# Four Mamba-style layers on one core: images in pairs, convolution by planes through DRAM, outputs in groups of two chunks

## The chip, the cores and the metric

The kernel runs on one core of one Trainium2 chip, in float32 throughout. The metric is the device time of one launch in microseconds, the median of three runs. One core has TensorE (PE: matrix products, with its weight loads shown as PEld), VectorE (DVE), ScalarE (ACT), GpSimd (POOL) and SyncE (SP, which issues the DMA transfers here). Each engine runs its own instructions strictly in the order of its program; engines wait for one another through semaphores.

## The reference, cut to what matters

Four images of 64x64 positions and 192 channels go through four layers a, b, c, d. Each layer is a group normalisation, then a selective state-space block, then an addition to the layer's input:

```python
# per layer, one image; L = 64*64 = 4096 positions, 16 states
xn = group_norm(x)                       # 32 groups of 6 channels
u, z = in_proj(xn)                       # 192 -> 384 + 384 (layer c: 192 + 192)
u = silu(depthwise_conv(u) + bias)       # a: 4 taps along the sequence; b, c, d: 3x3
for each direction:                      # a: 4, b: 1, c: 4 (two at a time), d: 4
    s = u in this direction's order      # rows, rows reversed, columns, columns reversed; b: snake
    dt, B, C = x_proj(s)
    delta = softplus(dt_proj(dt) + b)
    h = exp(delta*A)*h + (delta*s)*B     # a recurrence along the sequence, 16 states a channel
    y += (h*C).sum(states) + D*s
# b, c, d: y = layer_norm(y over channels) * silu(z);  a: each direction's y * silu(z of that direction)
x = x + out_proj(y)
```

Layer a has its own input and output projection for each of its four directions, and its output passes a last linear map, which the kernel folds into the output weights. The next layer's group normalisation needs the mean and variance of the whole new x, so a layer of an image cannot start before the same image's layer before it has ended. Different images do not depend on each other at all.

## The kernel before

An image is held as channels on partitions (two halves of 96 channels, 4096 positions along the free axis) and worked on in 8 chunks of 512 positions. Images run one after another, and in each the layers a, b, c, d. Each layer has three parts, in scopes of memory pools that open and close one after the other:

**In** (`stats`, `load_normal`, then `conv1d` for a, `conv` for b, c, d). `stats` turns moments gathered earlier into mean and rstd (two small PE products, one Ln and one Exp on ACT). x is loaded in 8 chunks and normalised on DVE (line 122). For each block of channels PE makes `pu` (lines 175, 231), ACT copies it into a padded plane `pad` (179, 235), and DVE adds the taps: a first `tensor_scalar` and one `scalar_tensor_tensor` for each further tap (159 and 161; 261 and 263). Of the first block some chunks are done on PE instead, as products with diagonal matrices (`pc`, 198 and 253): 6 of 8 chunks for b and d, 5 for c, 2 for a. ACT applies Silu. In b and d the result `xc` stays in SBUF for the scans; in a it is stored to DRAM (`xd_a`, one store for each block), in c in both row and column order from SBUF tiles `xc` and `xt` (line 1016); column order is made in SBUF, so that each run of memory stored is 16 KB.

**Scans** (`scans`). An order written out by hand and pinned by `keep` runs over directions, chunks and pairs of states: `p_px` (413), `p_dbl` (420), a store and broadcast loads of B and C, `p_softplus`, `p_du` (485), `inflow` (588, POOL), `decay` (582 and 584, ACT), `scan` (633, DVE), `outflow` (648, POOL or DVE), `total` (688, PE), `store` (702 and 706). Chunks of xs are loaded from DRAM where the source is there; otherwise `p_px` and `p_du` read `xc` directly, with a stride for column directions.

**Out** (`out0` for a, `output` for b, c, d). `output` makes a first pass over all 8 chunks (load y, for c add two parts; `bn_stats` and `bn_aggr` at 798 and 799; load and normalise x; products `pz` at 807, Silu at 810 into z), then one rsqrt for all chunks, held behind all the Silus by `behind`, and then a second pass over the 8 chunks: normalise y (821), transposes `pg` (828), scale and bias on ACT (838), product with z on POOL (839), products `po` (846), addition of x (850), store, moments for the next group normalisation (70). `out0` is one pass over 8 chunks, each with four directions of `pz` (963), Silu (967), `pg` (970), product on DVE (974) and `po` (931).

Outside `scans` the order of each engine's instructions is made by the scheduler of the framework, which goes by the order in which they are recorded and by when their operands and buffers come free.

Of the kernel before, what the change touches and what calls it, by code (L numbers as in the profile page):

```python
# [27 lines left out]
CONV_ROWS = 16  # L28
CONV_SPLIT = 37
# [17 lines left out]
class Net:  # L47
# [24 lines left out]
    def new_moments(self, key):  # L72
        return self.const.tile([HP, 2, NCH, 6], F32, tag="mom", bufs=2, name=f"mom_{key}")
# [12 lines left out]
    def stats(self, keep, pool, pp, st, key):  # L86

        nc = self.nc
# [3 lines left out]
        ps = pp.tile([HP, 2], F32, tag="gps", bufs=1, name=f"gm_{key}")  # L92
        nc.tensor.matmul(ps, self.gmat, mv[:, :, 0], start=True, stop=True)
        mean = keep.tile([HP, 2], F32, tag="mean", name=f"mean_{key}")
# [6 lines left out]
        ps = pp.tile([HP, 2], F32, tag="gps", bufs=1, name=f"gv_{key}")  # L101
# [3 lines left out]
        rstd = keep.tile([HP, 2], F32, tag="rstd", name=f"rstd_{key}")  # L105
# [23 lines left out]
    def conv(self, pool, pp, xn, xc, sums, P, nb, w_u, cpack, taps, shape, interior, borders, snake, key, xt=None):  # L129

        nc = self.nc
        k = len(taps)
        r0, c0 = interior
        wu = pool.tile([HP, 2, nb * P], F32, tag="wu", name=f"wu_{key}")
        nc.sync.dma_start(wu, w_u)
        cp = pool.tile([P, nb, cpack.shape[-1]], F32, tag="cp", name=f"cp_{key}")
        nc.sync.dma_start(cp, cpack)

        def silu(b, lo, hi, v):
            bias = cp[:, b, k : k + 1]
            o = img(xc[:, b, :])[:, lo:hi, :]
            if snake:
                nc.scalar.activation(o[:, 0::2, :], v[:, 0::2, :], AF.Silu, bias=bias)
                return nc.scalar.activation(o[:, 1::2, ::-1], v[:, 1::2, :], AF.Silu, bias=bias)
            if xt is not None:
                o2 = xt[:, b, :].rearrange("p (w h) -> p h w", h=H)[:, lo:hi, :]
                nc.scalar.activation(o2, v, AF.Silu, bias=bias)
            return nc.scalar.activation(o, v, AF.Silu, bias=bias)  # L150

        done = []

        def on_vector(b, pad, lo, hi):
            acc = img(sums[:, b, :])[:, lo:hi, :]
            for i, (tr, tcol) in enumerate(taps):
                v = pad[:, tr + lo : tr + hi, tcol : tcol + W]
                if i == 0:
                    nc.vector.tensor_scalar(acc, v, cp[:, b, :1], None, ALU.mult)
                else:  # L160
                    nc.vector.scalar_tensor_tensor(  # L161
                        acc, v, cp[:, b, i : i + 1], acc, ALU.mult, ALU.add
                    )
            done.append(silu(b, lo, hi, acc))

        for b in [*range(1, nb), 0]:
            pad = pool.tile([P, *shape], F32, tag="pad", bufs=nb, name=f"pad_{key}{b}")
            for sl in borders:  # L170
                nc.gpsimd.memset(pad[(slice(None), *sl)], 0.0)
            for ch in range(NCH):
                pu = pp.tile([P, T], F32, tag="pu", bufs=4, name=f"pu_{key}{b}{ch}")
                for h in range(2):
                    nc.tensor.matmul(
                        pu, wu[:, h, b * P : (b + 1) * P], xn[:, h, ch * T : (ch + 1) * T],
                        start=h == 0, stop=h == 1,
                    )
                nc.scalar.copy(pad[:, r0 + ch * R : r0 + (ch + 1) * R, c0 : c0 + W], rows(pu))
            if b:  # L180

                half = H // 2 - 1 - snake
                on_vector(b, pad, 0, half)
                on_vector(b, pad, half, H)
                continue
            diag = pool.tile([P, k, P], F32, tag="diag", name=f"dg_{key}")
            nc.vector.tensor_tensor(
                diag,
                self.ident[:P, None, :P].to_broadcast([P, k, P]),
                cp[:, b, :k, None].to_broadcast([P, k, P]),  # L190
                ALU.mult,
            )
            own = 6 if nb > 2 else 5
            on_vector(b, pad, own * R, H)
            for ch in range(own):
                pc = pp.tile([P, T], F32, tag="pc", bufs=3, name=f"pc_{key}{ch}")
                for i, (tr, tcol) in enumerate(taps):
                    nc.tensor.matmul(
                        pc, diag[:, i, :],
                        pad[:, tr + ch * R : tr + (ch + 1) * R, tcol : tcol + W],  # L200
                        start=i == 0, stop=i == k - 1,
                    )
                done.append(silu(b, ch * R, (ch + 1) * R, rows(pc)))
        return done

    def conv1d(self, pool, pp, xn, out, w_u, cpack, cols, rev, key):


        nc = self.nc
        P, nb = 128, 3  # L210
        wu = pool.tile([HP, 2, nb * P], F32, tag="wu", bufs=2, name=f"wu_{key}")
        nc.sync.dma_start(wu, w_u)
        cp = pool.tile([P, nb, 5], F32, tag="cp", bufs=2, name=f"cp_{key}")
        nc.sync.dma_start(cp, cpack)
        taps = [6 - k if rev else k for k in range(4)]
        done = []
        for b in range(nb):
            pad = pool.tile([P, (H + 6) * W], F32, tag="pad", bufs=4, name=f"pad_{key}{b}")
            if cols:
                pad = pad.rearrange("p (h w) -> p h w", w=W)  # L220
                inside = pad[:, 3 : H + 3, :]
                borders = pad[:, :3, :], pad[:, H + 3 :, :]
            else:
                pad = pad.rearrange("p (h w) -> p h w", h=H)
                inside = pad[:, :, 3 : W + 3]
                borders = pad[:, :, :3], pad[:, :, W + 3 :]
            nc.gpsimd.memset(borders[rev], 0.0)
            for ch in range(NCH):
                pu = pp.tile([P, T], F32, tag="pu", bufs=5, name=f"pu_{key}{b}{ch}")
                for h in range(2):  # L230
                    nc.tensor.matmul(
                        pu, wu[:, h, b * P : (b + 1) * P], xn[:, h, ch * T : (ch + 1) * T],
                        start=h == 0, stop=h == 1,
                    )
                nc.scalar.copy(inside[:, ch * R : (ch + 1) * R, :], rows(pu))
            acc = pool.tile([P, L], F32, tag="acc", bufs=2, name=f"acc_{key}{b}")
            xo = pool.tile([P, L], F32, tag="xo", bufs=2, name=f"xo_{key}{b}")
            to = xo.rearrange("p (w h) -> p h w", h=H) if cols else img(xo)
            bias, r0 = cp[:, b, 4:5], 0
            if b == 0:  # L240
                r0 = CONV_ROWS
                diag = pool.tile([P, 4, P], F32, tag="diag", bufs=2, name=f"dg_{key}")
                nc.vector.tensor_tensor(
                    diag,
                    self.ident[:, None, :].to_broadcast([P, 4, P]),
                    cp[:, b, :4, None].to_broadcast([P, 4, P]),
                    ALU.mult,
                )
                for r in range(0, r0, R):
                    pc = pp.tile([P, T], F32, tag="pc", bufs=2, name=f"pc_{key}{r}")  # L250
                    for i, t in enumerate(taps):
                        v = pad[:, t + r : t + r + R, :] if cols else pad[:, r : r + R, t : t + W]
                        nc.tensor.matmul(pc, diag[:, i, :], v, start=i == 0, stop=i == 3)
                    done.append(nc.scalar.activation(to[:, r : r + R, :], rows(pc), AF.Silu, bias=bias))

            for lo, hi in ((r0, CONV_SPLIT), (CONV_SPLIT, H)):
                a = img(acc)[:, lo:hi, :]
                for i, t in enumerate(taps):
                    v = pad[:, t + lo : t + hi, :] if cols else pad[:, lo:hi, t : t + W]
                    if i == 0:  # L260
                        nc.vector.tensor_scalar(a, v, cp[:, b, :1], None, ALU.mult)
                    else:
                        nc.vector.scalar_tensor_tensor(a, v, cp[:, b, i : i + 1], a, ALU.mult, ALU.add)
                done.append(nc.scalar.activation(to[:, lo:hi, :], a, AF.Silu, bias=bias))
            nc.sync.dma_start(out[:, b, :], xo)
        return done

    def conv2d(self, pool, pp, xn, xc, sums, P, nb, w_u, cpack, snake, key, xt):
# [5 lines left out]
            snake, key, xt,  # L274
        )

    def keep(self, ins):

# [890 lines left out]
```

## Time and profile before

| | |
|---|---|
| runs | 30956.24, 30958.65 and 30989.16 us; median 30958.65 us |
| profiled execution | span 30966.4 us, 7.7 us above the median |
| busy share of the span | PE 76%, PEld 57%, DVE 84%, ACT 75%, POOL 79% |
| scan stage of a, b, c, d, first image | 2190.5, 571.9, 1146.0, 2283.2 us |
| from the last scan of a layer to the first scan of the next: a to b, b to c, c to d, d to a | 551.8, 290.8, 263.5, 443.6 us |
| before the first scan of all, after the last scan of all | 306, 152 us |
| DMA | mean 108 GB/s; 1371014 packets, 187576 of them under 512 bytes |

A span is the time from the first to the last instruction of the one execution that was profiled. The busy share of an engine is an average over very different stages: the table's two rows of stages say more. A gap between two scan stages holds one layer's out and the next layer's in, one after the other, and a lead-in of the next scans.

### The profile page before, as it was taken

How to read it: one execution, taken by the hardware profiler on the slowest of the kernel's cores; microseconds unless marked ns; L12 is line 12 of the kernel's file. 1: busy time of each engine (PE TensorE's matmuls, PEld its weight loads, DVE VectorE, ACT ScalarE, POOL GpSimd, SP SyncE). 2: the span in 40 equal slices, each digit the busy share in tenths (PEclk: the TensorE clock that was granted, in tenths of full speed). 3: DMA queues.
4: the chain of work that ended last, by engine and by line, in shares of the span. 5: the costliest groups of instructions: out<-in, count | busy, mean ns of one | idle time of the engine just before them, and what ended most of it. 6: DMA issues, size and time to landing. Idle time of an engine off the chain costs nothing. (4 is left out here: it accounts for less than half of the span.)

```text
span 30966.4 us, 377424 instructions
## 1 busy us (share of the span) xinstructions
PE 23496.1 (76%) x134728; PEld 17601.4 (57%) x134728; DVE 26106.5 (84%) x17436; ACT 23185.8 (75%) x45261; POOL 24377.8 (79%) x13726
## 2 busy tenths in 40 slices
PE   7778777777777877777777787777777778777777
PEld 4664565665466456566546645656655664565665
DVE  8995788998899578899889957889988995788998
ACT  7883686887788368688778836868877883696887
POOL 5992696998599269699869926969986992696998
PEclk8889888888888888888888898888888889888888
DMA  3332343333333234333333323433333332343333
GB/s 116 117 118 81 98 113 104 104 113 114 113 117 118 80 99 113 103 104 113 114 113 118 118 80 99 114 103 104 111 115 115 117 116 81 100 114 101 105 111 112
DMA packets 1371014, 3330.55 MB, mean 108 GB/s; under 512 B 187576, under 2 KB 635432, under 8 KB 1361448
## 3 DMA queue, kind: packets, MB, share of 16 engines
q1 hardware_dynamic: 1369128, 3306.40, 34.8%
q8 instruction: 1063, 17.42, 0.2%
q14 instruction: 823, 6.74, 0.1%
HBM read 2825.66 MB, written 480.25 MB: 107 GB/s over the span
## 5 line engine op out<-in xcount | busy, mean ns | idle before, releaser
L688 PE MATMUL py_d<-ident,c_d 128*128 128x128 f32 x24576 | 3853.0, 313 | 1636.6 <-DVE c_d L648 1106.2
L688 PE MATMUL py_a<-ident,c_a 128*128 128x128 f32 x24576 | 3723.2, 308 | 1616.7 <-DVE c_a L648 1304.1
L648 POOL TENSOR_TENSOR c_a<-h_a,C_a 128x1024 f32<-128x1024 f32 x1920 | 4511.3, 2368 | 330.5 <-DVE h_a L633 296.0
L648 POOL TENSOR_TENSOR c_d<-h_d,C_d 128x1024 f32<-128x1024 f32 x1920 | 4507.1, 2362 | 165.2 <-issue 128.9
L688 PEld LDWEIGHTS py_d<-ident,c_d 128*128 128x128 f32 x24576 | 3326.5, 163 | 2184.6 <-DVE c_d L648 1060.9
L688 PEld LDWEIGHTS py_a<-ident,c_a 128*128 128x128 f32 x24576 | 3251.7, 160 | 1972.9 <-DVE c_a L648 1413.3
L633 DVE TENSOR_TENSOR_SCAN h_d<-dAs_d,carry_d,ut_d 128x1024 f32<-128x1024 f32 x1536 | 3546.9, 2336 | 404.4 <-PE ut_d L611 264.8
L588 POOL TENSOR_TENSOR u_d<-du_d,B_d 128x1024 f32<-128x1024 f32 x1536 | 3643.7, 2372 | 0.0
L588 POOL TENSOR_TENSOR u_a<-du_a,B_a 128x1024 f32<-128x1024 f32 x1536 | 3622.3, 2376 | 0.3
L633 DVE TENSOR_TENSOR_SCAN h_a<-dAs_a,ut_a 128x1024 f32<-128x1024 f32 x1536 | 3430.6, 2273 | 227.6 <-PE ut_a L611 215.4
L633 DVE TENSOR_TENSOR_SCAN dA_d<-dA_d,carry_d,u_d 128x1024 f32<-128x1024 f32 x1152 | 2692.7, 2337 | 298.6 <-ACT dA_d L584 298.2
L633 DVE TENSOR_TENSOR_SCAN dA_a<-dA_a,u_a 128x1024 f32<-128x1024 f32 x1152 | 2623.0, 2277 | 381.1 <-ACT dA_a L584 381.1
L582 ACT ACTIVATE dA_d<-delta_d,A_d 128x512 f32<-128x512 f32 (+1 forms) x3072 | 2122.7, 691 | 952.6 <-DVE h_d L633 697.8
L582 ACT ACTIVATE dA_a<-delta_a,A_a 128x512 f32<-128x512 f32 x3072 | 2124.0, 691 | 828.9 <-DVE h_a L633 593.7
L688 PE MATMUL py_c<-ident,c_c 128*128 128x128 f32 x12288 | 1909.7, 312 | 936.0 <-DVE c_c L648 689.8
L611 PE MATMUL ut_d<-ident,dut_d 128*128 128x128 f32 x12288 | 2101.5, 297 | 378.5 <-ACT dut_d L602 272.7
L648 POOL TENSOR_TENSOR c_c<-h_c,C_c 128x1024 f32<-128x1024 f32 x960 | 2253.2, 2362 | 154.2 <-issue 106.5
L611 PE MATMUL ut_a<-ident,dut_a 128*128 128x128 f32 x12288 | 1888.3, 299 | 614.3 <-ACT dut_a L602 349.0
L602 ACT ACTIVATE dut_d<-duT_d,BT_d 128x384 f32<-128x384 f32 x4096 | 2316.8, 606 | 0.0
L688 PEld LDWEIGHTS py_c<-ident,c_c 128*128 128x128 f32 x12288 | 1661.9, 163 | 1142.3 <-DVE c_c L648 672.3
L602 ACT ACTIVATE dut_a<-duT_a,BT_a 128x384 f32<-128x384 f32 x4096 | 2293.2, 605 | 0.3
L611 PEld LDWEIGHTS ut_d<-ident,dut_d 128*128 128x128 f32 x12288 | 1603.3, 162 | 1001.5 <-issue 388.2
(379 smaller groups left out, 57835.9 us busy)
## 6 DMA issues: line engine op xcount, KB each, us to landing
C_a<-bc_a SPq DMA_DIRECT2D x1024, 512.0 KB
C_d<-bc_d SPq DMA_DIRECT2D x1024, 512.0 KB
B_a<-bc_a SPq DMA_DIRECT2D x512, 512.0 KB
C_c<-bc_c SPq DMA_DIRECT2D x1024, 256.0 KB
B_d<-bc_d SPq DMA_DIRECT2D x512, 512.0 KB
C_b<-bc_b SPq DMA_DIRECT2D x256, 512.0 KB
B_c<-bc_c SPq DMA_DIRECT2D x512, 256.0 KB
xd_a<-xo_a SPq DMA_DIRECT2D x48, 2048.0 KB
```

The lines of the kernel that those rows point to most:

```text
L582: keep(nc.scalar.activation(out, delta, AF.Exp, scale=o.A[:, t.b, k : k + 1]))
L588: keep(nc.gpsimd.tensor_tensor(t.u, t.c.du[:, t.b, None, :].to_broadcast([P, NT, T]), t.c.B[t.j], ALU.mult))
L602: keep(nc.scalar.activation(o[:, :, g, :], i[:, :, g, :], AF.Copy, scale=c.BT[:, q, g, n : n + 1]))
L611: keep(nc.tensor.matmul(t.u[:, n, q * 128 : (q + 1) * 128], t.c.scaled[t.n0 + n][:, q, t.b * P : (t.b + 1) * P], self.ident, start=q == 0, ...
L633: keep(nc.vector.tensor_tensor_scan(hf, af, uf, initial, ALU.mult, ALU.add))
L648: keep(engine.tensor_tensor(t.cm, t.h, t.c.C[t.j], ALU.mult))
L688: keep(nc.tensor.matmul(c.py[b][:, q, :], t.cm[:, n, q * 128 : (q + 1) * 128], self.ident[:P, :P], start=first, stop=last and q == TB - 1 ...
```

## The change

**Order of images.** Images go in pairs: a of image 0, a of image 1, b of image 0, b of image 1, and so on to d of image 1, then the same for images 2 and 3. Between two scan stages a function `between` opens one set of pools, records `enter` (the in of the layer whose scans come next) and then `leave` (the out of the layer whose scans have just ended). These two belong to different images. The DRAM tiles for x between layers are doubled. The moments of images 0 and 1 are both gathered at the start; d of images 0 and 1 gathers those of images 2 and 3.

**Convolution.** One function, `plane`, replaces `conv` and `conv1d`. It does one block of channels at a time in pieces of at most 36 rows: `pu`, the padded plane, taps on DVE, or on PE for the first `OWN` chunks of block 0. `OWN` depends on the pair of layers that meet. Every piece is stored to DRAM from SBUF. Where an order by columns is wanted (a: two directions, c, d) ACT writes the piece turned into `xt`, and the store puts it down in runs of as many positions as the piece has rows: 36 or 28 positions, 144 or 112 bytes, 8192 runs a store. All scans load xs from DRAM; the views of `xc` are gone.

**Outputs.** `output` works on groups of two chunks: first pass, rsqrt, second pass, then the next group. Each group's rsqrt has its own Ln and Exp.

**Buffers.** Both parts share SBUF and the 8 PSUM banks: `pu` 4 or 5 to 2, `pc` 3 or 2 to 1, `pad` 3 or 4 to 2, `pz` 3 to 2 (b, c, d), `py` 3 to 2 (b, c, d) and 2 to 1 (a), `po` 2 to 1, `g`, `gn`, `gr` 2 to 1, and in a `yt` 6 to 3, `go` 3 to 2.

```diff
+PIECE = 36
+GROUP = 2
+OWN = {"a": 2, "b": 6, "c": 5, "d": 6, "aa": 0, "ab": 0, "bb": 8, "bc": 5, "cc": 5, "cd": 8,
+       "dd": 8, "da": 3, "bd": 8}
...
+    def plane(self, pool, pp, x, key, P, w_u, cpack, taps, shape, corner, borders, own, stores):
...
+        for ch in range(NCH):
+            pu = pp.tile([P, T], F32, tag="pu", bufs=2, name=f"pu_{key}{ch}")
...
+            nc.scalar.copy(pad[:, r0 + ch * R : r0 + (ch + 1) * R, c0 : c0 + W], rows(pu))
...
+        lo = 0
+        while lo < H:
+            by_pe = lo < own * R
+            hi = min(lo + PIECE, own * R if by_pe else H)
+            acc = pool.tile([P, PIECE, W], F32, tag="acc", bufs=2, name=f"acc_{key}{lo}")[:, :n, :]
...
+                    t = pool.tile([P, PIECE * W], F32, tag="xt", bufs=2, name=f"x{order}_{key}{lo}")
...
+            for order, store in stores:
+                for to, part in store(lo, hi):
+                    nc.sync.dma_start(to, tiles[order][part])
+            lo = hi
...
     def output(self, pool, pp, P, nb, outs, wz, wo, ln, snake, x_src, norm, dst, x_next, key):
...
+        for g0 in range(0, NCH, GROUP):
...
+            for ch in range(g0, g0 + GROUP):
...
+            with self.behind(gates):
+                self.rsqrt(pool, r, v, [128, nq, 1], kg)
+            for ch in range(g0, g0 + GROUP):
...
+        def turned(src, b):
+            v = src[:, b, :].rearrange("p (w h) -> p w h", h=H)
+            return lambda lo, hi: [(v[:, :, lo:hi], ())]
...
+    def between(self, last, S, dp):
...
+            nc.scalar.preload_act_table_set(NLE)
+            done = []
+            if S:
+                done = self.enter(S, ip, pp, dp, OWN[(last.name if last else "") + S.name])
+            if last:
+                last.after.st = self.leave(last, op, pp)
+        return done
...
+        order = [
+            stages[im, l]
+            for pair in range(0, NB, 2) for l in range(len(layers))
+            for im in range(pair, min(pair + 2, NB))
+        ]
```

## The prediction

> **What bounds the kernel now.** I read the page's busy shares first, then the busy time by stage, then the instruction groups of the gaps.
>
> ```profile
> span 30966.4 us, 377424 instructions
> PE 23496.1 (76%) x134728; PEld 17601.4 (57%) x134728; DVE 26106.5 (84%) x17436; ACT 23185.8 (75%) x45261; POOL 24377.8 (79%) x13726
> ```
>
> No engine is full on average. By stage of the first image (columns: stretch, length, busy time of PE, PEld, DVE, ACT, POOL, clock, DMA share, GB/s):
>
> ```profile
> 306.00:2496.50 2190.50, 1636.99 (x10828) 1370.71 (x10828) 2056.19 (x1062) 1890.08 (x3391) 2108.24 (x894) 0.88 0.35 115
> 2496.50:3048.30 551.80, 493.80 (x1460) 234.06 (x1460) 196.85 (x222) 108.56 (x180) 14.45 (x24) 0.94 0.26 76
> 3620.20:3911.00 290.80, 191.52 (x498) 81.61 (x498) 132.50 (x210) 92.00 (x136) 48.33 (x44) 0.81 0.43 108
> 5057.00:5320.50 263.50, 186.00 (x456) 78.34 (x456) 167.27 (x233) 69.73 (x99) 34.15 (x40) 0.83 0.34 88
> 5320.50:7603.70 2283.20, 1766.41 (x11160) 1410.53 (x11160) 2118.58 (x1344) 1935.48 (x3895) 2207.66 (x1374) 0.87 0.34 108
> 7603.70:8047.30 443.60, 327.03 (x796) 141.80 (x796) 263.70 (x280) 173.69 (x207) 52.71 (x43) 0.85 0.38 123
> ```
>
> The scans (rows 1 and 5) keep POOL and DVE over 92% busy. Four images of 2190, 572, 1146 and 2283 us are 24,760 us, and the change leaves their order alone. What it works on is the gaps: 4x552, 4x290, 4x265, 3x444, 306 at the start and 152 at the end, together some 6,210 us. In a gap out and in follow each other, each with another engine in front:
>
> ```profile
> 2501.00:2901.00 400.00, 385.17 (x1200) 185.66 (x1200) 96.71 (x144) 62.48 (x110) 0.00 (x0) 0.98 0.29 88
> 2901.00:3020.00 119.00, 90.71 (x208) 40.14 (x208) 99.36 (x74) 33.42 (x52) 1.29 (x12) 0.88 0.14 33
> 3624.60:3762.50 137.90, 103.13 (x288) 46.14 (x288) 64.51 (x149) 41.39 (x78) 34.47 (x24) 0.88 0.45 122
> 7609.00:7756.20 147.20, 107.21 (x288) 45.95 (x288) 59.58 (x149) 35.58 (x53) 36.30 (x24) 0.85 0.52 135
> 7756.20:8005.60 249.40, 200.24 (x452) 86.85 (x452) 203.28 (x128) 124.60 (x134) 3.11 (x12) 0.91 0.30 112
> 8005.60:8047.30 41.70, 15.68 (x36) 6.75 (x36) 0.84 (x4) 11.68 (x17) 10.70 (x5) 0.54 0.46 157
> ```
>
> These are out of a (PE), in of b (DVE), outs of b and d (chains in which nobody is full), in of a (DVE and PE), and the lead-in of scan a, a chain of load, `px`, `dbl`, store, broadcast, softplus, `du`. With a full overlap only the busiest engine of each gap would count, so the prize is real: out d with in a needs PE for 307 of 397 us.
>
> **But the built order does not overlap much.** Engines are in order, so the order of the built program counts. `between` records `enter` first, and the scheduler puts it first. Of DVE's out instructions, those ahead of the last in instruction are 12 of 144 (a then a), 5 of 144 (a then b), 38 to 64 of 164 or 172 in the others, and these are the `bn_stats` and x chunks of the first one or two groups. Of PE's, 82 of 792, 22 of 792, and 0 to 2 (20 for d then a). So in runs nearly alone, then out. I sum each gap as: in + what is left of out + lead-in, against the same three parts before.
>
> ```profile
> L839 POOL TENSOR_TENSOR g_b<-g_b,z_b 128x512 f32<-128x512 f32 x24 | 34.5, 1463 | 100.7 <-ACT g_b L838 86.5 <-issue 14.3
> L807 PE MATMUL pz_b<-gn_b,wz_b 96*128 96x512 f32 x96 | 44.7, 630 | 17.0 <-DMA gx_b<-x 17.0
> L198 PE MATMUL pc_c<-pad_c,dg_c 96*96 96x512 f32 x90 | 38.8, 592 | 0.0
> L161 DVE SCALAR_TENSOR_TENSOR cs_c<-pad_c,cp_c,cs_c 96x2112 f32<-96x2112 f32 x8 | 19.3, 2407 | 0.0
> ```
>
> *Out in groups.* The built order puts a group's `pz` behind the `po` of the group before, with one `po` and one `g` buffer. A group is then: 6 `pz` of 4 instructions, 44.7/96 each, 11 in all; z; two table loads at 1.28 with Ln and Exp, and four small DVE steps, 5 together; then two chunks of transposes, three scales on ACT (1.1 in b), three POOL products at 1.46 and `po`, 10.5 each: about 40 us. Four are 160 against 138 and 147. c has two blocks: 30 a group. On ACT the rsqrt stands behind the group's six Silus and ahead of the next group's; on SP the next loads of x stand behind the stores of `gr`, which wait for `po`. So a group is not fetched past the one before it.
>
> *In by planes.* a with `OWN` 0 moves 8 `pc` chunks of PE to DVE: 12 planes x (36 rows: 2304 positions at 1.14 ns, three times, + 2.0; 28 rows: likewise 7.8) = 17.7 x 12 = 212, + 9 normalising + the 46 in which DVE waited in the row above (249 - 203), and more, since pads fell from 4 to 2: 276 to 304, I take 290 for 249. b with `OWN` 0: 3 x 40 + 54 = 165 to 175 for 119. With `OWN` 8, block 0 comes first and is all PE: 8 `pu` (14) and 8 `pc` (90 instructions are 5 chunks of 18; 38.8/90 x 18 = 7.7 each) are 77 us before DVE has its next pad; then 80 of DVE, and 12 to 18 of stats and loads at the start: 169 to 175 against 119 and 124. With 5 for c: 116 to 144 against 92. On SP each plane's stores, which wait for ACT, stand ahead of a later plane's weights.
>
> *Lead-in.* 28 us where `xc` was in SBUF becomes 33 with xs loaded (42 in a, 56 in c with its stores): +5 for b, +5 for d, -20 for c.
>
> The gaps, after against before (out + in + lead-in):
> - a-a: 290 + 7 chunks of 46.5 (out a's (400 - 28)/8) + 42 = 657 against 691. One `po` and one `py` buffer add up to 2 a chunk: -25.
> - a-b: 170 + 360 + 33 = 563 against 552: +8.
> - b-b: 169 + 20 (rest of the first group) + 120 + 33 = 342 against 285: +57.
> - b-c: 130 + 140 + 33 = 303 against 290: +12.
> - c-c: 130 + 105 + 33 = 268 against 254: +15.
> - c-d: 173 + 105 + 33 = 311 against 265: +47.
> - d-d: 175 + 16 + 120 + 33 = 344 against 299: +45.
> - d-a, once: 273 + 117 + 42 = 432 against 444: -13.
>
> Two of each and one d-a: 2 x 159 - 13 = +305. The start has 16 more `bn_stats` and plane's smaller buffers: +15; the last out, in groups: +12. Work taken away inside the scans:
>
> ```profile
> L485 POOL TENSOR_TENSOR du_d<-delta_d,xc_d 128x1536 f32<-128x1536 f32 x31 | 119.0, 3839 | 4.7 <-ACT delta_d L442 4.7
> ```
>
> This is a mean of 3.43 on row chunks and 4.20 on column chunks; from loaded xs all are 3.43. 64 x 0.77 = 49 us on POOL, the scan's bound: -50 (0 to -50). Extra xs loads (768 KB a chunk at 34% DMA share) hide.
>
> *Turned stores* are what no row shows: 8192 runs of 144 or 112 bytes to DRAM, 512 an engine. Nearest rows: the trace's packet records have 176-byte loads at 15 ns (384 of them land in about 0.55 us, 23 ns a run and engine), and 768-byte stores at 36 ns with five times the bytes. So 7.7, 11.8 or 18.4 us a store. The column planes of a make one each 8.9 us of DVE, 12 per image: below 8.9 hidden, else (11.8 - 8.9) x 12 = 35, or 113 an image. I take 19 ns, between the small-run rows: 0.8 x 12 x 4 = +38. In d (6 stores in 175 us) and c they hide but for the last. Bounds: 0 to +450.
>
> The Trainium skill ("DMA: Bandwidth & Descriptors", Specifications) says that a transfer under 512 B makes the DMA engine read, modify and write. No run here shows a store that short; were a run thereby twice the 15 ns row, an estimate from this page's rule, a's stores would be 15.4 us and add 310, where the row alone adds none.
>
> Sum against the profiled execution: 305 + 15 + 12 - 50 + 38 = +320, so 30,966 + 320 = 31,286, and 7.7 less for the median: about **31,280 us**, 1.0% slower.
>
> **Rivals.** (F) *Overlap as named*: the scheduler's order leaves waits that the other image fills. For it: x and the moments are ready at the scan's end, so the 17 us in which PE waited for `gx` and the start of in are covered; if the groups run into each other at PE's 26 us each (103/4) instead of 40, each b and d gap loses 40 and each c gap 25, and a's out loses its start. Then b-b 300, c-d 285, d-d 302, b-c 263, c-c 243, a-a 630, a-b 540: 2 x (15 + 20 + 3 - 27 - 11 - 61 - 12) = -146, d-a -60, -50 of `du`, -40 for in's own starts (3 us in each of 15 gaps): about 30,660. Against it: the built order. It decides from a group time of 30 us down.
> (S) *Stores bound*: at 36 ns a run and no hiding, a's ins become a DMA queue: 305 + 15 + 12 - 50 + 455 + 50 for tails in c and d = 31,750; each further 10 ns a run adds 61 x 4 = 245.
> (N) *Nothing moves*: groups cost what the passes did and starts are covered, gains in a pay for b to d: 30,960. Under 0.2% (62 us) a measurement cannot tell it from no change.
>
> **How the numbers follow.** My forecast 0.45 (its own range 31,080 to 31,500), S 0.20, N 0.07, F 0.28. Faster is F, 0.28; same 0.07; slower 0.65. Leaving a tenth at each end cuts F at its better half, 30,600, and S beyond 45 ns, 31,950.
>
> **What would show it.** Right: out's `pz` beginning only when in's last `scalar_tensor_tensor` ends; b-b, c-d and d-d gaps of 310 to 345 us; four idle notches of PE in each out; DVE idle some 75 us after a b or d scan; `du_d` at 3.43. Wrong: gaps b-b or d-d under 285; PE over 80% busy between scans; or a's in over 330 us with DMA near full in its second half, which is S.

## The result, and the profile after

The changed kernel took 32,069.4 us (median of four runs, 32,061.2 to 32,076.0) against 30,957.4: the ratio is 1.0355, 95% interval 1.034 to 1.037. It is slower, as forecast, but by 1,112 us and not 320, outside the range. First the page of the profile after (span; busy time by engine; DMA packets).

```profile
span 32059.4 us, 379003 instructions
PE 23692.7 (74%) x134812; PEld 17761.5 (55%) x134812; DVE 26066.5 (81%) x17586; ACT 23478.6 (73%) x45488; POOL 24321.7 (76%) x13726
DMA packets 2202386, 3532.01 MB, mean 110 GB/s; under 512 B 942009, under 2 KB 1398953, under 8 KB 2193577
```

Every engine has about the work it had; the span has grown around it. Packets under 512 bytes went from 187,576 to 942,009. Not all new runs are 144 or 112 bytes: where PE does a share of block 0, the pieces are cut there too, and the trace also has stores of 16, 48, 64 and 96 bytes a run, 114,688 runs of 745,472. Now busy time by stretch: the first gap, then a-a, a-b, b-b, c-d and d-a, and last a scan of d (columns as in the prediction's tables: stretch, length, busy time of PE, PEld, DVE, ACT, POOL, clock, DMA share, GB/s).

```profile
0.00:415.30 415.30, 235.60 (x488) 100.03 (x488) 213.98 (x163) 140.70 (x149) 15.80 (x23) 0.81 0.90 97
2606.00:3304.40 698.40, 588.13 (x1640) 270.48 (x1640) 300.98 (x270) 204.65 (x254) 16.72 (x19) 0.91 0.64 99
5490.20:6040.60 550.40, 454.57 (x1352) 216.25 (x1352) 222.86 (x229) 107.77 (x171) 14.51 (x24) 0.89 0.30 90
6610.40:6970.00 359.60, 245.21 (x602) 108.29 (x602) 153.46 (x233) 102.23 (x169) 44.21 (x48) 0.82 0.29 87
10501.70:10871.00 369.30, 224.47 (x511) 93.89 (x510) 152.87 (x240) 107.29 (x129) 34.80 (x40) 0.75 0.61 101
15860.40:16410.40 550.00, 381.56 (x828) 159.90 (x828) 249.19 (x294) 195.73 (x227) 48.18 (x43) 0.80 0.75 99
13578.10:15860.40 2282.30, 1733.73 (x11160) 1420.90 (x11160) 2118.57 (x1344) 1936.11 (x3894) 2195.24 (x1374) 0.86 0.38 118
```

Apart from a-a and a-b no engine is busy for even 70% of a gap, so a sum of waits sets these lengths; and where column order is stored (rows 1, 2, 5, 6) the DMA share is 0.61 to 0.90. All scans together take 24,777 us, before 24,747; all gaps 7,283, before 6,220. So the gaps carry 1,063 of the 1,093 us between the two spans. The other 30 are mostly one scan of d that took 2,314 us where its three fellows took 2,282 to 2,286; why is open.

| gap, us | first | a-a | a-b | b-b | b-c | c-c | c-d | d-d | d-a | last |
|---|---|---|---|---|---|---|---|---|---|---|
| forecast: the gap before plus the stated change | 321 | 666 | 560 | 342 | 302 | 269 | 312 | 344 | 431 | 164 |
| changed kernel, first profile | 415 | 698 | 550 | 360 | 347 | 328 | 369 | 421 | 550 | 190 |
| changed kernel, measured again | 392 | 676 | 552 | 359 | 343 | 328 | 358 | 412 | 524 | 187 |

### The profile page after: what moved, and what is told of

Its sections match the earlier page's. It is cut to its first block, busy times and chain, and to the rows that moved or that the text cites. A ratio compares the mean times of both kernels' runs of the same rounds, so it can differ in the third digit from the quotient of the medians.

```text
span 32059.4 us, 379003 instructions
## 1 busy us (share of the span) xinstructions
PE 23692.7 (74%) x134812; PEld 17761.5 (55%) x134812; DVE 26066.5 (81%) x17586; ACT 23478.6 (73%) x45488; POOL 24321.7 (76%) x13726
```

## The experiments

Three theories at the start: (1) the short runs of the turned stores hold the DMA engines; (2) the order of recording puts in first and out behind it; (3) the buffers and the groups make out long. The gaps of a profiled execution are the finer measure; a time without an interval is that of one execution. The kernel before took 30,961 to 30,970 beside them.

**Long runs in place of short ones.** The columns hold positions in another order, so a, c and d compute with other data.

```diff
-            v = src[:, b, :].rearrange("p (w h) -> p w h", h=H)
-            return lambda lo, hi: [(v[:, :, lo:hi], ())]
+            return lambda lo, hi: [
+                (src[:, b, lo * W : hi * W].rearrange("p (w h) -> p w h", w=W), ())
+            ]
```

> The changed kernel with every turned store written in runs of one piece (36 or 28 rows of 256 bytes) in place of 144 or 112 bytes: same number of stores, same bytes, same tiles, ACT still turns; the columns then hold positions in another order, so layers a, c, d compute with other data. Theory 1, short runs (each store of 8192 runs holds the 16 DMA engines about 19 us): the ins fall back to what DVE and PE need, first gap 415 to about 330, a-a 698 to 660, d-a 550 to 475, b-c and c-c 347 and 328 to about 305 and 290, c-d and d-d 369 and 401-421 to about 320 and 355: some 550 us less in all, about 31,500. Theory 2, order and groups (in first, then out group by group, is what costs): within 60 us of 32,060. Theory 3, buffers (pu, pad and acc too few): the same within 60 us.

31,599 us, gaps 6,845. First gap 337, a-a 636, b-c 333, c-c 318, c-d 342, d-a 482; b-b, whose stores were never turned, 359 as before the edit. The busy strip of the DMA engines, in 40 slices of the first gap, for the changed kernel and then for this one:

```profile
DMA  8979300505051404046999999999999999994281
DMA packets 129073, 40.40 MB, mean 97 GB/s; under 512 B 118893, under 2 KB 121209, under 8 KB 128296
```

```profile
DMA  7996930015023061500606122060434032063380
DMA packets 16175, 40.39 MB, mean 120 GB/s; under 512 B 4205, under 2 KB 6521, under 8 KB 14630
```

The same megabytes, and the half in which columns are stored is a wall of nines only with short runs. What waited for a DMA in the first gap of the changed kernel (us in total, times, longest): weights of later planes, whose loads stand behind the stores, and the next scan's first product:

```profile
PE px_a L346 <- DMA xs_a<-xd_a: 64.9, 1, 64.9
PE pu_a L150 <- DMA wu_a<-in_a_in: 37.0, 3, 13.4
DVE acc_a L206 <- DMA cp_a<-in_a_conv: 32.5, 2, 16.7
```

And with long runs, where DVE no longer waits for `cp_a`:

```profile
PE px_a L346 <- DMA xs_a<-xd_a: 30.1, 1, 30.1
PE pu_a L150 <- DMA wu_a<-in_a_in: 13.0, 1, 13.0
```

Theory 1 holds for the places that it named. It was expected to give back 550 us and gave 470 against the first measurement, 315 against the changed kernel measured again (below).

**Short runs alone, in the kernel before.** Each finished column plane of layer a goes out in two stores.

```diff
-            nc.sync.dma_start(out[:, b, :], xo)
+            if cols:
+                for lo, hi in ((0, 36), (36, H)):
+                    nc.sync.dma_start(
+                        out[:, b, :].rearrange("p (w h) -> p w h", h=H)[:, :, lo:hi],
+                        xo.rearrange("p (w h) -> p w h", h=H)[:, :, lo:hi],
+                    )
+            else:
+                nc.sync.dma_start(out[:, b, :], xo)
```

> The kernel before, with the one store of a finished column plane in layer a split in two along the rows, 36 and 28 rows, so that each puts down 8192 runs of 144 or 112 bytes (24 planes, 48 such stores in the whole kernel); nothing else changes and the data are the same. Theory 1: 48 stores at about 19 us against 18 us of DVE for a plane: each in of a grows by some 75 to 115 us, 300 to 450 in all, 31,260 to 31,400. If such stores hide behind DVE (15 ns a run, the row I predicted from): under 60 us, and DMA under 50% busy in that half of in.

31,159 us: 189 more, less than the 300 expected and three times the 60 of the rival. The in of each image grew by 47 us (d-a 490 for 444). While the queue was full, from 190 to 310 us, the 16 engines got through 80,496 packets, one every 23.9 ns an engine:

```profile
DMA packets 80496, 10.31 MB, mean 86 GB/s; under 512 B 80496, under 2 KB 80496, under 8 KB 80496
```

At that pace a store of 512 runs an engine takes 12.2 us, 3.3 more than the 8.9 us of DVE beside it: 40 us for the 12 stores of an image, of the 47 measured. What the scan's first product waited for in the first gap, in the kernel before and with this edit:

```profile
PE px_a L413 <- DMA xs_a<-xd_a: 38.8, 1, 38.8
```

```profile
PE px_a L420 <- DMA xs_a<-xd_a: 78.0, 1, 78.0
```

It waits twice as long, in one piece, while the stores drain.

**The changed kernel again**, beside the edited ones.

> The changed kernel as it is, beside the others on this chip, since its first gap (no out in it) was 415 us in the first profile and 391 to 394 in four of the edited kernels that leave layer a's in alone. If the rate of short runs differs from chip to chip: first gap about 393, a-a 675, the kernel 31,750 to 31,950. If the edits had shortened it: 415 and 32,060 again.

31,914 us, first gap 392, a-a 676. The packet record of a run of 144 bytes lasts 27 ns on average here and 33 in the first profile, one of 112 bytes 36 and 42, while a 176-byte load lasts 15 to 16 in both. These records overlap: from 210 to 330 us, with the queue full, their sum in the first profile is 157% of the time of 16 engines. So the pace is the better figure: packets in these 120 us, in the first profile and here, 25.9 and 22.6 ns a packet and engine.

```profile
DMA packets 74170, 8.06 MB, mean 67 GB/s; under 512 B 73593, under 2 KB 74169, under 8 KB 74169
q1 hardware_dynamic: 74169, 8.04, 157.2%
```

```profile
DMA packets 84792, 9.35 MB, mean 78 GB/s; under 512 B 84214, under 2 KB 84790, under 8 KB 84790
```

The two measurements lie 155 us apart, 135 of it in the gaps, and there where columns are stored: so some 135 to 155 us of the 1,112 go with a slower pace of short runs in the first one. The first gap is 391 to 394 in all the edits below that leave layer a's stores alone, on two further chips; they are set against this run.

**Out recorded first.**

```diff
-            if S:
-                done = self.enter(S, ip, pp, dp, OWN[(last.name if last else "") + S.name])
             if last:
                 last.after.st = self.leave(last, op, pp)
+            if S:
+                done = self.enter(S, ip, pp, dp, OWN[(last.name if last else "") + S.name])
```

> The changed kernel with leave recorded ahead of enter, nothing else. Theory 2: out then runs from the scan's end as in its own scope (b 160, d 165, c 110 us) and in fills the waits of PE and DVE, so that b-b falls from 360 to 230-290 and the kernel to 30,700-31,300. Theory 1: the turned stores go on setting when in ends in a, c and d; only a-b and b-b gain, under 200 us in all, 31,850 or more. If the scheduler's order is without weight: within 60 us.

31,859 us, only 55 better than the changed kernel measured again, so theory 2's 30,700 to 31,300 is missed. The number is theory 1's (31,850 or more), but a-b did not gain as it says. b-b fell to 331 and c-c to 303, but a-a rose to 735 and a-b to 582. Out now ends early (b: 185 us after the scan) and the in's taps come behind it, at 207 to 292. Turned round, the order still puts one side behind the other.

**No overlap: two scopes, out and then in.**

> The changed kernel with two scopes in place of one: leave in its own pools, then enter in its own, other layers' order and all buffers as they are. If the shared scope hides much work (theory: overlap works, it only pays for other things), each of the 15 gaps grows by 60 us or more, 33,000 and over. Theory 2 says that little of out lies beside in (5 to 82 of some 800 instructions), so the gaps grow by 0 to 40 us each: 32,060 to 32,600.

32,593 us, gaps 7,847. That is 699 us of gaps over the changed kernel measured again, 47 each in 15 gaps, just beyond the 40 of theory 2. So the shared scope did hide something, but the parts themselves, with their short stores and one after the other, had become 1,627 us longer than before.

**The same with the old buffers in `output`** (pz 3, py 3, po 2, g 2, gn 2, gr 2, nx its own).

> The kernel with two scopes in place of one (out, then in) and, in output for b, c and d, the buffers of the kernel before (pz 3, py 3, po 2, g 2, gn 2, gr 2, nx of its own); groups stay at two chunks. Theory B: outs of b and d fall from 185 to about 150 us, the last gap from 190 to 155, the kernel from 32,593 to about 32,200. Theory G: the last gap stays over 178 and the kernel over 32,480.

32,406 us; the last gap 180 for 190. Between the theories: the old buffers give back some 10 us in the last gap and 17 a gap in the eleven others with such an out. The last gap stays 28 over the kernel before, and the groups are what is left of the change there.

**Groups of four chunks, one y and one z.**

> The changed kernel with outputs in groups of 4 chunks (2 groups in place of 4) and one buffer of y and z in place of two, the same memory. Theory G (what a group costs is its rsqrt barrier, with tables, between a first and a second pass that do not overlap): the last out falls from 190 to about 165 us, and the b, c and d gaps by 15 to 25 us each, 31,800 to 31,900. Theory B (the buffers cut to one po, one g, one gr set the pace of a chunk): the last out stays within 5 us of 190 and the kernel within 60 us of 32,060.

31,717 us, but the last gap is 186 and b-b 358: unmoved, as theory B has it; b-c, c-c, d-d and d-a lost 18 to 30 and c-d 10, as theory G has it. The edit changed two things, since with one y a group's loads wait for the group before, and does not tell them apart.

**Block 0 last, 6 chunks on PE.**

```diff
-        for b in range(nb):
+        for b in [*range(1, nb), 0]:
```

> The changed kernel with block 0 as the last of the planes in layers b, c, d (as in the kernel before) and its PE share back at 6 of 8 chunks in b-b, c-d and d-d. If DVE's late start (85 to 101 us after the scan) is what lengthens the ins of b, c and d: DVE's first tap at 35 to 50 us, b-b from 360 to about 325, c-d and d-d 30 less, b-c and c-c 15 to 25 less, 31,800 to 31,900 in all. If out, which comes after, or the stores set the end anyway: within 60 us of 32,060.

31,708 us: b-b 336, c-d 339, d-d 370, c-c 305. DVE's first tap began at 34 to 40 us, where it was 83 to 100. Against the changed kernel measured again, b-c and c-c, where only the order of the blocks changed, are 13 to 27 us shorter; b-b, c-d and d-d, where the share of PE changed too, 19 to 42.

**Column order made in SBUF, one store a plane**, with the data in the right order.

```diff
+            whole = pool.tile([P, L], F32, tag="xw", bufs=2, name=f"xw_{key}")
+            whole = whole.rearrange("p (w h) -> p w h", h=H)
...
+                    tiles[order] = whole[:, :, lo:hi]
...
+        for order, store in stores:
+            if order == "col":
+                for to, part in store(0, H):
+                    nc.sync.dma_start(to, whole[part])
```

> The changed kernel with column order made in SBUF for a whole plane (16 KB a partition, two buffers) and one store of it in long runs; all scans get the data of the reference. Theory 1: as with the run of long runs in wrong order, 31,600 within 80 us, a-a 636, d-a 482, c-d 342. Rival: the plane's one store now follows its last Silu, and the scan's first load waits for 2 MB more: 10 us more in each gap of a, c and d, about 31,750.

31,682 us, gaps 6,889: theory 1's 31,600 and 80 more. The gain is in a and d: b-c (350) and c-c (328) are no shorter than with short runs, where the wrong order had 333 and 318. The last tap of c's in ends at 168 to 171 us again, in the wrong order at 157 to 164; why is open. Still 669 us of gaps over the kernel before, with nothing turned in DRAM. What is left belongs to order, groups, shares and buffers.

**In turns.** `enter`, `plane`, `leave`, `output` and `out0` became generators, and `between` steps the one that is less far. A group's first pass stands ahead of the second pass of the group before; pieces have even lengths (with 40 rows on PE the change left a sliver of 4); block 0 is last; shares are new.

```diff
+            while sides:
+                side = min(sides, key=lambda x: x[1] / x[2])
+                side[1] += 1
+                if next(side[0], self) is self:
+                    sides.remove(side)
...
+        late = None
+        for g0 in range(0, NCH, GROUP):
+            now = yield from first(g0)
+            if late:
+                yield from second(*late)
+            late = (g0, *now)
+        yield from second(*late)
...
+OWN = {"a": 2, "aa": 0, "ab": 0, "bb": 3, "bc": 2, "cc": 3, "cd": 5, "dd": 3, "da": 0}
```

> The changed kernel with enter and leave recorded in turns (a piece of a plane, then a chunk of out, by their shares), a group's first pass recorded ahead of the second pass of the group before, column order made in SBUF and stored in long runs, block 0 last, pieces of even length, and PE shares set so that PE and DVE come out even (b-b 3, b-c 2, c-c 3, c-d 5, d-d 3, d-a 0 chunks). Buffers stay as the change has them. Theory 2 (the order was what lost the overlap): b-b about 250, b-c and c-c 230-250, c-d and d-d 270-290, a-a 610, a-b 480, d-a 400: 30,300 to 30,600, faster than the kernel before. Theory B (two images on one po, g, gr, gn and two pz and pu: a wait of one side now holds the other's work on the same engine): gaps like long runs in right order or longer, 31,300 to 31,800.

30,624 us, and timed in rounds:

> The in_turns kernel unchanged, timed against the kernel before: 30,620 within 30 us against 30,960, ratio about 0.989. If its one look was a lucky execution: a ratio above 0.995.

30,613 us against 30,964: ratio 0.9886, 95% interval 0.987 to 0.9903, faster by 1.1%. Its a-a, a-b, b-b, c-d, d-d and d-a:

```profile
2514.30:3147.00 632.70, 573.35 (x1640) 264.09 (x1640) 299.51 (x271) 203.20 (x254) 16.76 (x19) 0.95 0.34 110
5333.70:5824.30 490.60, 445.53 (x1352) 209.72 (x1352) 220.66 (x229) 107.49 (x171) 14.53 (x24) 0.94 0.33 101
6395.80:6676.60 280.80, 204.15 (x494) 86.28 (x494) 185.56 (x251) 99.28 (x161) 60.37 (x48) 0.82 0.36 112
10037.80:10322.70 284.90, 191.91 (x456) 79.30 (x456) 167.45 (x248) 106.02 (x126) 48.36 (x40) 0.78 0.43 131
12611.40:12906.40 295.00, 202.12 (x499) 84.77 (x498) 183.98 (x251) 114.06 (x137) 60.01 (x48) 0.83 0.45 138
15189.00:15577.80 388.80, 300.53 (x732) 128.80 (x732) 276.10 (x291) 188.17 (x214) 75.03 (x43) 0.89 0.43 140
```

In a-a and a-b PE is now busy for 91% of the gap, with its lead-in of over 30 us inside; in b-b DVE works 186 of 281 us where it worked 153 of 360. Three more runs take this gain apart:

> The in_turns kernel with the change's PE shares (8 chunks in b-b, c-d, d-d; 5 in b-c, c-c; 3 in d-a) and block 0 first again; recording in turns, groups' first passes ahead, even pieces and long runs stay. If the order of recording is what gained: 30,650 to 30,950, with b-b, c-d and d-d 10 to 30 us longer than 283, 286 and 296. If the shares were the gain: 31,300 or more.

31,002 us, gaps 6,236, some 380 more than in turns, and so no faster than the kernel before: the shares and block 0 last, which I had put at 10 to 30 us in the b and d gaps alone, are worth 37 to 57 in b-b, c-d and d-d and 18 to 24 in b-c, c-c and d-a.

> As in_turns_old_shares, but enter is recorded whole and then leave, as the change does; a group's first pass still stands ahead of the second pass of the group before. If taking turns is what gained: b-b back to about 330, the last gap 160, the kernel 31,300 to 31,500. If the passes of the groups, out of step, were the gain: under 31,100, b-b under 300.

31,201 us, better than the 31,300 expected; gaps 6,410. Taking turns is thus worth 175 us, two thirds of it in a-b (548 to 491, twice); b-b, c-d and d-d even lose 3 to 10 as long as block 0 comes first, since DVE's first tap then falls back to 131 to 141 us, from 78 to 86. From long runs in the right order (6,889) to here are 478 us for two edits: passes out of step and even pieces. Where only the one acts, the last gap went from 190 to 158; where only the other, the first gap went from 339 to 328.

> The in_turns kernel with two buffers of g in output in place of one. If the single g (ACT writes the next chunk's only when po of the chunk before has read it) sets the pace: b-b, b-c, c-c, d-d 8 to 20 us shorter each, the last gap 160 to 150, 30,400 to 30,520. If in, beside it, is what ends last: within 40 us of 30,620.

> The in_turns kernel with two buffers of g, timed against the kernel before: 30,530 within 30 us against 30,960, ratio about 0.986. If its one look was a lucky execution: a ratio of 0.9886 or more, as in_turns had.

30,534 us, and 30,561 timed, ratio 0.9871 (0.9855 to 0.9888). The intervals of this and of in turns overlap; the gaps of the timed profiles are 5,786 and 5,853. So one g seems to cost 50 to 70 us, less than the 100 expected, and the times alone do not show it clear of noise.

## Why the prediction was right and wrong

**Right.** The built order was the thing to read. In b-b the last tap ended 169 us after the scan; the first group's products stood before that and the other three groups behind it, to 322, where the sum had 169 + 20 + 120 = 309. DVE began 83 to 100 us after the scan, for 75. a-b came out at 551 for 560. (Its parts, 563, are 11 over 552 and not 8, a slip that moves nothing.) The `du_d` step itself was exact:

```profile
L410 POOL TENSOR_TENSOR du_d<-delta_d,xs_d 128x1536 f32<-128x1536 f32 x128 | 440.1, 3438 | 93.3 <-ACT delta_d L375 93.2
```

Of the 1,093 us between the profiled spans 320 were forecast. The other 773 are the stores (438 by the gaps that long runs give back, for 38), the scans (+30 for -50) and 293 in the ins and outs themselves.

**Wrong, the largest term: the turned stores, +38.** Two steps failed. The price: I took 19 ns a run, 0.8 us a store beyond the DVE work that hides it. With a full queue the pace was 25.9 ns in the first profile and 22.6 in the second, so 4.4 and 2.7 us a store, 210 and 130 us by the prediction's own sum; long runs gave back 270 and 177 in the gaps of a. The nearest of my rows was the landing of the 176-byte loads, 23 ns or 11.8 us a store. The place: in c and d I had them hidden but for the last, and priced that at nothing; there long runs gave back 168 and 125 us. This is rival S's mechanism, and its place in a was right (DMA full in the second half of a's in, which ran to 345 and 327 us); 303 to 438 us of gaps stand against its 505. The Trainium skill's rule ("DMA: Bandwidth & Descriptors", Specifications: below 512 B a read, modify and write) gave an estimate of 30 ns, where the packet records last 27 to 42 on average. The size is near; that a read before the write is the cause is not shown by any run.

**The out in groups: 40 us a group was right, what stands around the groups was not.** In b-b the first `po` of each group starts 40, 41 and 40 us after the one before:

```profile
6794.53 4.66 PE L774 MATMUL po_b<-g_b,wo_b 128*96 128x512 f32 x6 [0.24 <-POOL g_b L767]
6834.53 5.13 PE L774 MATMUL po_b<-g_b,wo_b 128*96 128x512 f32 x6 [0.28 <-POOL g_b L767]
6875.78 5.00 PE L774 MATMUL po_b<-g_b,wo_b 128*96 128x512 f32 x6 [0.29 <-POOL g_b L767]
6915.65 3.84 PE L774 MATMUL po_b<-g_b,wo_b 128*96 128x512 f32 x6 [0.28 <-POOL g_b L767]
```

The three groups behind the in took 202 to 322 us, the 120 of the sum. But the first group still needed 33 us after the last tap, for 20: PE stopped in the middle of its products for 31 us, until ACT had done Silus of the in, and the rsqrt and the second pass came after that. The lead-in took 37 for 33. In the last gap I set four groups, 160, against 147 for an out of before that holds 19 us of loads ahead of its first product. The groups took 161 from the first `pz` to the last `po` (the two passes of before 124), and 24 stood ahead of them: 190 for 164. Who waited for whom from the end of in to the end of out in b-b, and PE's stop in the first group:

```profile
POOL g_b L767 <- ACT g_b L766: 172.4, 8, 67.3
DVE gr_b L778 <- PE po_b L774: 60.7, 16, 6.8
DVE rsq_b L84 <- ACT r_b L83: 36.0, 4, 9.7
ACT g_b L766 <- PE po_b L774: 30.3, 4, 8.1
PE pz_b L735 <- ACT xsnake_b L165: 31.0, 1, 31.0
```

Inside the 40 the parts were others than I had summed. DVE waits 9 us for the rsqrt in each of the four groups (36.0), where I had 5 for all of it, since Ln stands behind the group's last Silu and a table load of 1.28 us precedes Ln and Exp each. ACT waits 8 us a group for `po` to free the one `g`, which the sum left out. That the total came out at 40 is partly luck. Passes out of step took the last gap from 190 to 158, a second g to 153, what it was in the kernel before.

**Wrong: the in of c, 130 us.** The last tap ended at 168 to 171. For b and d I had DVE wait for block 0 on PE; for c, with 5 chunks on PE and first in line too, I did not. Its first tap began at 90 to 100 us. b-c and c-c are 45 and 59 us over the forecast, of which long runs gave back 10 to 14. In a-a the parts were too dear: 636 with long runs, for 666, which hid some of the stores' cost there.

**Wrong: -50 us of `du` in the scans of d.** POOL's time fell from 489.5 to 440.1 us over 128 chunks, and the second scan of d kept its length: 2,281 before, 2,282 after, with POOL busy 2,207 and then 2,195 us. What POOL gained it spent waiting. I had called POOL the scan's bound from a busy share of 96%. That DVE, at 93% beside it, holds the pace as much is my reading; no run tests it.

**The rivals.** F's condition was wrong: as the change is recorded, few waits are filled (47 us a gap), and a group took 40 us, where 30 was to decide. A time near its 30,660 came only from another kernel, with long runs, turns, passes out of step and work for DVE from the start (30,613); that the two numbers are close is luck, as F also counted 50 us of `du` that never came. S was the nearest, 31,750. Its store term was 67 to 202 us too large, and the ins, the outs and the scans bring the other 366 to 386. I gave it 0.20 because I took a rate of loads for that of stores. Of the signs, the gaps of b-b, c-d and d-d (360 to 421) lie above the 310 to 345 named, and `pz` did not wait for the in's last tap: the first group's began at 93 to 128 us.

## What to carry to other kernels

Putting two independent pieces of work into one scope overlaps little by itself when each engine's order is fixed: read the built order, and record the two in turns, with shares that let each engine start at once and finish together. Price a short store by its number of runs and the pace with a full queue, not by the length of one record, and ask what is queued behind it; long runs paid here in a and d, even though ACT has to turn the data first. When a busy engine loses work and its neighbour is within a few per cent as busy, do not count on the gain.

## What the runs showed of the hardware that I had not expected

The packet records of short store runs overlap and spread widely: in the changed kernel's first profile those of 144 and 112 bytes last 33 and 42 ns on average and 16 and 18 in the median. The shorter run lasts longer in both measurements of the changed kernel (42 and 33 ns, 36 and 27), but not in the kernel before with short runs (35 and 36), so the length alone is not the reason. The same program's short runs went at 25.9 ns a packet and engine in one measurement and at 22.6 in another, while its 176-byte loads lasted the same (15 to 16 ns). Why is open; the chip of the first measurement is not known. The granted TensorE clock was lower where PE waited for the stores: 0.81 in the first gap of the changed kernel, 0.88 with long runs, 0.90 in the kernel before.
